# The sums over four states in the body's scan move from the decay's tile to a tile of their own

## The chip, the cores and the metric

The kernel runs on one core of a Trainium2 chip, in one launch. The metric is device time in microseconds (us), the median of several runs; lower is better. The core's engines work in parallel and wait for each other through semaphores: TensorE (PE; its weight loads are listed apart as PEld), VectorE (DVE), ScalarE (ACT), GpSimd (POOL), and SyncE (SP), whose queue issues all DMAs of this kernel. Each engine and each queue works in the order in which the program lists its instructions.

## What is computed

Two layers of a perceiver-like stack over 8 batches of 64 rows of width 512, in float32, with a context of 1601 rows per batch. The scan that the change touches is the second block, a state space model ("mamba"):

```python
    x = x + _L0_xattn_ref(_layernorm(x, axis=-1), ctx_4096, ...)
    x = x + _L0_attn_ref(_layernorm(x, axis=-1), ...)      # the scan
    x = x + _L0_ffn_ref(_layernorm(x, axis=-1), ...)
    x = x + _L1_xattn_ref(_layernorm(x, axis=-1), ctx_4096)
    x = x + _L1_attn_ref(_layernorm(x, axis=-1), ...)
    x = x + _L1_ffn_ref(_layernorm(x, axis=-1), ...)
```

and within `_L0_attn_ref`:

```python
        def step(state, inp):
            dt_t, B_t, C_t, u_t = inp
            dA = jnp.exp(dt_t[..., None] * A)
            state = state * dA + (dt_t * u_t)[..., None] * B_t[:, None, :]
            y = jnp.einsum('bdn,bn->bd', state, C_t)
            return (state, y)
...
        y = ys.transpose(1, 0, 2) + x * D
```

There are 1024 channels, 16 states per channel and 64 time steps per batch. The sum over states in `y` is what is stored elsewhere after the change.

## The kernel before

**Main stream.** The first cross attention (32 heads, 8 key heads) is most of the work. `x_all` (L527) walks over 64 units, one per batch and key head: keys (`k_ps`, L363), values (`v_ps`, L334), scores (`s_ps`, L385), running maximum on DVE (`mx`, L392, L390, L395), exponentials (DVE L426, ACT L427), weighted values (`o_ps`, L464), their scaling (L476 to L479), and for each pair of batches the output projection (`w_ps`, L521, added on DVE at L524). The keys leave PSUM through ACT L108 and DVE L109.

**Side chains.** The batches are grouped in pairs. When the first attention of a pair is done, a generator for the other five blocks of that pair starts (`chain`): mamba, `ffn`, `xattn1`, `attn1`, `ffn1`. The first three pairs' chains ("body") run beside the main stream; `advance` (L1328) draws from them in proportion to the main stream's progress, so the program text interleaves both. What a body chain records is pinned by `keep_in_program_order` (L65, the line that the profile gives to all of it): an edge places it behind the instruction recorded just before it on its engine. The main stream's own instructions are not pinned. A list scheduler then orders each engine's instructions by a timing model of its own, and gives tiles their buffers, within these edges. The last pair's chain runs after the main stream ("tail"), with other buffers and other code for the scan (`tail` branches); what is left of the third chain runs beside it.

**The body's scan.** `mamba` (L807) holds 8 tiles of 128 channels; `scan(c, sh, bc)` (L895) takes one tile `c` and four of the 16 states, so a chain has 4 x 8 = 32 scans, and the three body chains 96. One scan does, on tiles of 128 x 512 (four states x two batches x 64 steps):

1. ACT: four exponentials into `da`, the decay (L899); POOL: a memset of the first step of `da` (L900);
2. POOL: `h` = B x du (L905), with B from `bc`, which a DMA spreads over the partitions once for every eight scans (L885, one buffer);
3. DVE: the scan itself, over `da` and `h` into `h` (L909, TENSOR_TENSOR_SCAN);
4. DVE for even `c`, POOL for odd `c`: `h` times C (L911);
5. DVE: the sum over the four states (L914, TENSOR_REDUCE) into `y`, which is the first quarter of `da`;
6. DVE: the update of `u` with `y` (L915, SCALAR_TENSOR_TENSOR, shown as `lv<-lv,a` or `lv<-lv,c_Dp,a`).

`da` and `h` come from the tag `a2`, five buffers of 2 KB per partition in the body's pool `ca`. The profile shortens `a2` to `a`. The normalised and transposed input of mamba is also an `a2` tile and is read until the gates at the end of mamba. A buffer is given to the next tile when the last reader or writer of the old one is done, which for `da` is step 6 and for `h` step 5.

**The tail's scan** has no `y` tile; it adds the states on PE (L956).

The third chain's `xattn1` reads the context again: scores L1036 with loads of `ctxT` (L1033), transposes L1074, values L1092 with loads of `ctxN` (L1087, L1089).

Of the kernel before, what the change touches and what calls it, by code (L numbers as in the profile page):

```python
# [16 lines left out]
P = 128  # L17
D = 512
NC = 4
T = 64  # L20
# [22 lines left out]
CPLAN = (0, 1, 2, None, None, 3)  # L43
AVPLAN = ((), (), (0, 1, 2, 3), (4, 5, 6, 7), (8, 9, 10, 11), (12,))
EXPLAN = ((0,), (1, 2), (3,), (4, 5), (6,), ())
BUFS = {"a2": 5, "lv": 3, "bc": 1, "xpad": 1, "b2": 5, "b4": 2, "w2": 3, "xr": 2}
BUFS_TAIL = {"a2": 6, "du": 2, "bc": 2, "xpad": 4, "s4": 11, "kb": 3, "b2": 8, "b4": 3, "w2": 12, "xr": 2}


# [29 lines left out]
class Kernel:  # L79
# [13 lines left out]
    def sb(self, tag, shape, dt=FP, bufs=None, pool=None):  # L93
        if pool is None:
            pool, bufs = self.ca if tag in MAMBA_TAGS else self.cp, bufs or self.bufs.get(tag)
            if tag in REST and self.tp and not self.tail:
# [710 lines left out]
    def mamba(self, gi, x, xo):  # L807
# [40 lines left out]
        sm = self.sb("sm", [64, P], bufs=1)  # L848
# [36 lines left out]
        def bcast(sh):  # L885
            bc = self.sb("bc", [P, 2, HS, 2, T])
            for a in range(2):
                r = a * NST + sh * HS
                nc.sync.dma_start(
                    out=bc[:, a].rearrange("p s b t -> p (s b t)"),  # L890
                    in_=self.bc_s[gi][r : r + HS].rearrange("r t -> (r t)")[None, :].to_broadcast([P, HS * P]),
                )
            return bc

        def scan(c, sh, bc):  # L895
            da = self.sb(self.td, [P, HS, 2, T])
            for s in range(HS):
                k = sh * HS + s
                nc.scalar.activation(da[:, s], dt[:, c], AF.Exp, scale=self.A[:, c, k : k + 1])  # L899
            nc.gpsimd.memset(da[:, :, :, 0:1], 0.0)  # L900
            du = dus[:, c]
            if sh == 0:
                nc.gpsimd.tensor_tensor(du, dt[:, c], u[:, c], ALU.mult)
            h = self.sb(self.ts, [P, HS, 2, T])
            nc.gpsimd.tensor_tensor(h, bc[:, 0], du[:, None].to_broadcast([P, HS, 2, T]), ALU.mult)  # L905

            yield 1
            hf, df = h.rearrange("p s b t -> p (s b t)"), da.rearrange("p s b t -> p (s b t)")
            nc.vector.tensor_tensor_scan(hf, df, hf, 0.0, ALU.mult, ALU.add)  # L909
            yield 1  # L910
            (nc.gpsimd if c % 2 else nc.vector).tensor_tensor(h, h, bc[:, 1], ALU.mult)  # L911
            yield 1
            y = da[:, 0]
            nc.vector.tensor_reduce(y.rearrange("p b t -> p (b t)"), h.rearrange("p s b t -> p (b t) s"), AX.X, ALU.add)  # L914
            nc.vector.scalar_tensor_tensor(u[:, c], u[:, c], self.Dp[:, c : c + 1] if sh == 0 else 1.0, y, ALU.mult, ALU.add)  # L915
            yield 1

        wps = None
        if tail:
# [18 lines left out]
            for c in range(NCH):  # L938
                du = self.sb("du", [P, 2, T])
                nc.gpsimd.tensor_tensor(du, dt[:, c], u[:, c], ALU.mult)  # L940
                for k0 in range(0, NST, CS):
                    da = das[k0 // CS % 2]
                    for s in range(CS):
                        nc.scalar.activation(da[:, s, :, 1:], dt[:, c, :, 1:], AF.Exp, scale=self.A[:, c, k0 + s : k0 + s + 1])
                    bc, o = bcs[k0 // HS], k0 % HS
# [17 lines left out]
        else:  # L963
            for sh in range(nh):
                bc = bcast(sh)
                for c in range(NCH):
                    yield from scan(c, sh, bc)
# [332 lines left out]
    def run(self):  # L1300
        nc, tc, ctx = self.nc, self.tc, self.ctx
        nc.scalar.preload_act_table_set("natural_log_exp_and_others")
        self.setup(bufs=BUFS, accb=2, hs=4, tail=False, ahead=1, **TAGS)
        self.pc = ctx.enter_context(tc.tile_pool(name="pc", bufs=2, space=PSUM))
# [74 lines left out]
GROUPS = {8: [2, 2, 2, 2], 2: [2]}  # L1379
SPAN = [3.1,3.1,2.6,0.2]  # L1380
PREP_END = 2.8
MAMBA_TAGS = ("a2", "lv", "bc", "xpad", "sm")
FFN_TAIL = (("l", 0), ("l", 1), ("a", 0), ("l", 2), ("a", 1), ("d", 0), ("a", 2), ("d", 1), ("d", 2))
REST = {"w2":8,"b4":3}
OTB = 1
# [114 lines left out]
```

## Time and profile before

| what | us |
| --- | --- |
| median of three runs | 2729.16 (2728.2 to 2729.43) |
| the profiled execution, its own time | 2721.08 |
| its span, first to last instruction | 2719.3 |
| first body scan, first exponentials to last sums | about 752 to 1010 |
| second body scan | about 1397 to 1691 |
| third body scan | about 2028 to 2313 |
| last rows of the main stream's w_ps on PE | 2422 |

The mean granted clock of TensorE over the profiled execution is 0.977 of full speed. In the tables, "idle before, releaser" is the time for which an engine did nothing before an instruction, with the event that ended it; "x" is a number of instructions. A row of the view of time has its start and its length in us. The costliest instructions of the body's scan are, per instruction: TENSOR_TENSOR_SCAN 1603 ns (96 of them), TENSOR_REDUCE 1068 ns (96), the product with C on DVE 1115 ns (48), the update 487 ns (72) or 743 ns (24, those with D), and an exponential 392 ns on the page (384, all three chains).

### The profile page before, as it was taken

To read this page: it belongs to the slowest core of one execution; us is meant where nothing else is said; L and a number is where in the kernel's file an instruction comes from. 1 tells how busy PE (TensorE), PEld (TensorE's weight loads), DVE (VectorE), ACT (ScalarE), POOL (GpSimd) and SP (SyncE) were. 2 spreads that over 40 slices of the span, in tenths; PEclk is the share of its full clock that TensorE was granted. 3 is DMA by queue.
4 is the path that set the end of the run, shared out by engine and by line. 5 is a ranking of instruction groups with operands and counts; after the bars stand their busy time and mean duration, and the time that the engine had idled before them with its cause. 6 is when DMAs were issued, how large, how long until landed. Compare 5 with 4: busy or idle time off the path is not lost.

```text
span 2719.3 us, 43920 instructions
## 1 busy us (share of the span) xinstructions
PE 2565.7 (94%) x16288; PEld 2273.7 (84%) x16288; DVE 1746.8 (64%) x2843; ACT 1352.6 (50%) x3128; POOL 1171.4 (43%) x1123
## 2 busy tenths in 40 slices
PE   7999999999998899999999988999999998986888
PEld 6999999889887899978988987997897898964644
DVE  4544345577688886545568689544668879457854
ACT  4444554445565554544455554544555455445543
POOL 3212434464588643422357346421249445114610
PEclk9999999999999999999999998999999999997999
DMA  9544446665665234665234443565342463476575
GB/s 308 153 141 153 138 144 228 200 204 178 214 218 188 75 121 159 211 184 174 88 109 134 152 136 106 185 206 186 116 133 80 128 187 113 148 256 201 195 264 188
DMA packets 302934, 455.59 MB, mean 168 GB/s; under 512 B 80248, under 2 KB 179576, under 8 KB 298240
## 3 DMA queue, kind: packets, MB, share of 16 engines
q1 hardware_dynamic: 302720, 452.79, 52.2%
q8 instruction: 128, 2.10, 0.3%
q14 instruction: 86, 0.70, 0.1%
HBM read 380.23 MB, written 72.48 MB: 166 GB/s over the span
## 4 chain that ended last, share of the span: by engine, by line
PE 47%; DVE 11%; DMA 4%; POOL 3%; issue 3%; ACT 2%; POOLq 0%; DVEq 0%; ACTq 0%; SPq 0%
PE v_ps L334 10%; PE k_ps L363 10%; PE o_ps L464 6%; PE s_ps L385 5%; DVE a L65 4%; PE w_ps L521 2%; PE acc L819 2%; PE acc L777 2%; PE acc L774 1%; PE acc L1092 1%; PE acc L1036 1%; POOL a L65 1%; POOL ss L452 1%; DVE acc L953 1%; PE acc L1178 1%
## 5 line engine op out<-in xcount | busy, mean ns | idle before, releaser
L363 PE MATMUL k_ps<-cxb,wk 128*128 128x384 f32 x2304 | 473.5, 348 | 36.4 <-DVE kt L109 12.6
L334 PE MATMUL v_ps<-wv,cxb 128*128 128x256 f32 x3456 | 474.1, 283 | 7.4 <-DVE mx L392 3.9
L334 PEld LDWEIGHTS v_ps<-wv,cxb 128*128 128x128 f32 x3456 | 441.8, 190 | 28.9 <-issue 13.6
L363 PEld LDWEIGHTS k_ps<-cxb,wk 128*128 128x128 f32 x2304 | 406.8, 192 | 56.3 <-DVE kt L109 14.3
L385 PE MATMUL s_ps<-q,kt 128*128 128x256 f32 (+1 forms) x2496 | 414.5, 299 | 8.6 <-DVE mx L392 7.2
L464 PE MATMUL o_ps<-S,v 128*128 128x256 f32 (+1 forms) x1664 | 413.6, 381 | 2.6 <-DVE rw L479 1.7
L388 ACT COPY S<-s_ps 128x512 f32<-128x512 f32 (+1 forms) x448 | 242.5, 554 | 252.6 <-PE s_ps L385 249.0
L385 PEld LDWEIGHTS s_ps<-q,kt 128*128 128x128 f32 (+1 forms) x2496 | 342.0, 185 | 30.3 <-DVE mx L392 8.5
L392 DVE TENSOR_TENSOR mx<-s_ps,mx 128x512 f32<-128x512 f32 x256 | 175.4, 685 | 297.5 <-ACT S L388 297.2
L452 POOL TENSOR_TENSOR ss<-ss,S 128x512 f32<-128x512 f32 x254 | 356.6, 1404 | 14.9 <-ACT S L427 0.3
L429 POOL TENSOR_TENSOR ss<-S,S 128x512 f32<-128x512 f32 x64 | 84.0, 1312 | 640.0 <-ACT S L427 639.9
L464 PEld LDWEIGHTS o_ps<-S,v 128*128 128x128 f32 (+1 forms) x1664 | 299.4, 190 | 41.6 <-issue 5.6
L426 DVE TENSOR_TENSOR S<-S,m_ps 128x512 f32<-128x512 f32 (+1 forms) x448 | 257.5, 641 | 36.2 <-PE m_ps L412 35.4
L108 ACT ACTIVATE kt<-k_ps,c_bk 128x384 fp32r<-128x384 f32 (+1 forms) x256 | 151.8, 593 | 246.2 <-PE k_ps L363 245.4
L427 ACT ACTIVATE S<-S 128x512 f32<-128x512 f32 (+1 forms) x448 | 247.6, 600 | 41.4 <-DVE S L426 41.0
L109 DVE SCALAR_TENSOR_TENSOR kt<-k_ps,c_bk,kt 128x384 fp32r<-128x384 f32 (+1 forms) x256 | 160.9, 629 | 156.2 <-ACT kt L108 155.0
L337 ACT COPY v<-v_ps 128x256 f32<-128x256 f32 (+1 forms) x416 | 152.1, 368 | 195.8 <-PE v_ps L334 192.7
L334 PE MATMUL v_ps<-wv,cxt 128*128 128x256 f32 (+1 forms) x1536 | 211.3, 286 | 5.1 <-DVE mx L392 5.1
L334 PEld LDWEIGHTS v_ps<-wv,cxt 128*128 128x128 f32 (+1 forms) x1536 | 194.6, 176 | 17.3 <-issue 5.9
L363 PE MATMUL k_ps<-cxt,wk 128*128 128x450 f32 x768 | 179.3, 376 | 0.0
L65 DVE TENSOR_TENSOR_SCAN a<-a,a 128x512 f32<-128x512 f32 x96 | 153.9, 1603 | 32.2 <-POOL a L65 32.0
L65 ACT ACTIVATE a<-lv,c_A_log 128x128 f32<-128x128 f32 x384 | 122.8, 392 | 85.8 <-DVE a L65 84.8
(358 smaller groups left out, 3951.3 us busy)
## 6 DMA issues: line engine op xcount, KB each, us to landing
wo<-d_wo SPq DMA_DIRECT2D x96, 512.0 KB, 5.6
wk<-d_wk SPq DMA_DIRECT2D x63, 512.0 KB, 4.3
wv<-d_wv SPq DMA_DIRECT2D x31, 1024.0 KB, 5.7
cst<-in_ctxT_dram SPq DMA_DIRECT2D x96, 192.0 KB, 2.7
b<-in_ctxN_dram SPq DMA_DIRECT2D x36, 512.0 KB, 3.8
d_q<-q_t SPq DMA_DIRECT2D x32, 512.0 KB, 4.3
q<-d_q SPq DMA_DIRECT2D x64, 256.0 KB, 3.0
d_wo<-b SPq DMA_DIRECT2D x32, 512.0 KB, 2.9
```

The source lines that it names most:

```text
L65: return lambda *a, **k: self.tc.keep_in_program_order(f(*a, **k))
L109: eng.scalar_tensor_tensor(lo, src, bias, hi.bitcast(FP), ALU.add, ALU.subtract)
L334: nc.tensor.matmul(ps[:r], lhsT=cx[:, a, c, o : o + r], rhs=w[:, m, c, :], start=k == 0, stop=k == 11)
L337: nc.scalar.copy(vt[:r], ps[:r])
L363: nc.tensor.matmul(ps[:, :wd], lhsT=w[:, a, c, :], rhs=cx[:, m, c, :], start=k == 0, stop=k == 11)
L385: nc.tensor.matmul(sp[:r, gi, :], lhsT=kt[:, a, o : o + r], rhs=q[:, m, :], start=k == 0, stop=k == 2)
L388: nc.scalar.copy(s[:r, :n], sp[:r, :n])
L392: nc.vector.tensor_tensor(mx, sp, S[0] if len(S) == 1 else mx, ALU.max)
L426: nc.vector.tensor_tensor(sv, sv, ps[:r, 1:2].to_broadcast([r, w, 256]), ALU.add)
L427: nc.scalar.activation(sv, sv, AF.Exp, scale=ISC)
L452: nc.gpsimd.tensor_tensor(ss, ss, S[n], ALU.add)
L464: nc.tensor.matmul(ps[:, 0], lhsT=self.v[(b, j, t)][:r, hc : hc + P], rhs=S[t // 2][:r, t % 2], start=t == 0, stop=t == NT - 1)
```

## The change

The sum of step 5 goes into a tile `y` of its own, 128 x 2 x 64, with two buffers in the pool `ca`; the update reads it from there. `da` is then last read by the scan itself. The amount and form of the instructions stay as they are. The tail is not edited. The order that the scheduler finds, and the addresses, may differ anywhere after the first scan.

```diff
-BUFS = {"a2": 5, "lv": 3, "bc": 1, "xpad": 1, "b2": 5, "b4": 2, "w2": 3, "xr": 2}
+BUFS = {"a2": 5, "y": 2, "lv": 3, "bc": 1, "xpad": 1, "b2": 5, "b4": 2, "w2": 3, "xr": 2}
...
             (nc.gpsimd if c % 2 else nc.vector).tensor_tensor(h, h, bc[:, 1], ALU.mult)
             yield 1
-            y = da[:, 0]
+            y = self.sb("y", [P, 2, T])
             nc.vector.tensor_reduce(y.rearrange("p b t -> p (b t)"), h.rearrange("p s b t -> p (b t) s"), AX.X, ALU.add)
...
-MAMBA_TAGS = ("a2", "lv", "bc", "xpad", "sm")
+MAMBA_TAGS = ("a2", "y", "lv", "bc", "xpad", "sm")
```

`MAMBA_TAGS` lists the tags that come from the pool `ca`.

## The prediction

> **What bounds the kernel now.** I read the page first, then the stretches by engine, then the waits and the order of time inside the scans, and the end last. The page's first and clock lines:
>
> ```profile
> span 2719.3 us, 43920 instructions
> PE 2565.7 (94%) x16288; PEld 2273.7 (84%) x16288; DVE 1746.8 (64%) x2843; ACT 1352.6 (50%) x3128; POOL 1171.4 (43%) x1123
> PEclk9999999999999999999999998999999999997999
> ```
>
> TensorE (PE) is busy 94% of the span, and the work on it is the same before and after. So the edit can only move PE's idle time, 2719.3 − 2565.7 = 154 us, and the time lost to a lower clock. The waits of PE named in the view of time add up to 23 us in the first body scan (740 to 1010 us), 17 us in the dense half of the second (1600 to 1695), 15 us in the third (2028 to 2312), and some 70 us after 2400. Stretches of 10 us in the second scan and of 20 us near the end (columns: PE, weight loads, DVE, ACT, POOL busy with instructions, granted clock, DMA share, GB/s):
>
> ```profile
> 1610.00:1620.00 10.00, 5.34 (x30) 4.88 (x29) 6.83 (x7) 2.26 (x6) 4.16 (x6) 0.90 0.73 262
> 1660.00:1670.00 10.00, 4.99 (x19) 4.60 (x20) 9.93 (x12) 4.83 (x15) 3.94 (x5) 0.66 0.10 26
> 1670.00:1680.00 10.00, 7.49 (x51) 6.67 (x51) 10.00 (x15) 5.32 (x15) 4.40 (x5) 0.97 0.00 0
> 2420.00:2440.00 20.00, 14.08 (x89) 10.36 (x85) 8.59 (x25) 7.92 (x22) 0.42 (x6) 0.74 0.98 334
> ```
>
> Where the scan is dense, VectorE (DVE) is full and PE half idle; in the fourth row DMA is full. The waits of 1600 to 1695 us, and the rows around one sum over states:
>
> ```profile
> ACT a L65 <- DVE a L65: 37.6, 13, 7.5
> DVE a L65 <- POOL a L65: 9.0, 5, 3.5
> PE k_ps L363 <- DVE mx L392: 4.7, 1, 4.7
> 1616.09 1.22 DVE L65 TENSOR_TENSOR_SCAN a<-a,a 128x512 f32<-128x512 f32 x1
> 1617.23 1.01 DVE L65 TENSOR_REDUCE a<-a 128x128 f32<-128x512 f32 x1
> 1618.15 0.68 DVE L392 TENSOR_TENSOR mx<-s_ps,mx 128x512 f32<-128x512 f32 x1
> 1618.75 0.28 DVE L65 SCALAR_TENSOR_TENSOR lv<-lv,a 128x128 f32<-128x128 f32 x1
> 1618.95 1.04 DVE L65 TENSOR_REDUCE a<-a 128x128 f32<-128x512 f32 x1
> 1620.03 1.12 DVE L65 SCALAR_TENSOR_TENSOR lv<-lv,a 128x128 f32<-128x128 f32 x1
> 1618.33 1.28 ACT L65 ACTIVATE a<-lv,c_A_log 128x128 f32<-128x128 f32 x4 [7.52 <-DVE a L65]
> ```
>
> ACT's four exponentials start at 1618.33, when the sum (TENSOR_REDUCE) of 1617.23 ends. That is the wait which the edit touches. But PE's 4.7 us ended with mx at 1618.15, which stood on DVE behind the scan and the sum: PE lost by DVE's queue.
>
> **The change, part by part.** *Removed and added instructions:* none; 96 sums and 96 updates (SCALAR_TENSOR_TENSOR of lv) read and write another tile. y takes two buffers of 512 B.
>
> *(a) The decay's buffer comes free earlier: −3 us, bounds −6 and 0.* Of the five a2 buffers one holds the normalised input to the end of mamba, so two pairs of da and h are left. In the order of the old program 87 first exponentials take a buffer that a sum frees, and 93 products h = B·du one that DVE's update or scan frees. In the new one 91 exponentials take a buffer freed by a scan or update, and 66 products one freed by a sum. The exponentials may thus start a product and a sum earlier: 2.2 us (mean 1115 + 1068 ns), and h an update earlier. ACT's 37.6 us is no gain by itself: the chain of waits from 1595 to 1700 us holds ACT's exponentials once, for 1.29 us. What h's lateness costs DVE there is 9.0 us in five waits, of which 3.50 and 3.22 end with the load of bc, which stays single; 2.3 us remain. In 2200 to 2312 DVE waits 7.3 us for POOL, 2.6 of it behind bc. I take half of 2.3 + 4.7, about 3; all of it is 7, cut to 6 since PE does not lose every one.
>
> *(b) h meets the update on DVE: +2 us, bounds 0 and +4.* The update takes 0.28 us alone and 1.12 in the row above, where POOL runs too; 96 updates cost 52.8 us, 26 over 96 × 0.28, while the sums stay at 1.07 throughout. A product bound by the buffer used to start 0.08 us after the update; now it may start after the sum, and where a row of the main stream lies between sum and update (58 of 96 in the new order) the update can find POOL at work. I count some eight bound products in the trace; half of them at 1.0 us is 4, half of that 2.
> The Trainium skill, "SBUF — State Buffer" (Who interferes with whom), says that a DVE instruction with two SBUF inputs contends with a GpSimd instruction that reads SBUF, and that the one that issues first blocks the other, a reduction never. That speaks against the edit; the row's 0.84 us and the sums' constancy agree. By the page each late update would pay the rest of a 1.28 us product, 8 × 1.28 = 10 us by an estimate from it; the sum stays with the rows.
>
> *(c) The scheduler packs the scans closer: +8 us, bounds 0 and +12.* This is the largest term. With earlier buffers the built order puts side work ahead of main rows. Up to the second chain's end the order on DVE shifts by 0 to 7 rows, then by about 10, and in the third scan by 5 to 14. To price it I cut the 32 sums of a scan into groups of four and count the main rows of DVE in each, at the page's means. A group's own DVE work is 4 × (1.603 + 1.068 + 0.487) + 2 × 1.115 = 14.9 us. The main rows L392, L426, L109, L390, L395, L405, L476, L477, L479, L524 make 869 us over some 2340 us of the main stream, so PE at full pace asks for 0.37 us of them per us. A group with M us of main rows lasts at least M + 14.9 and lets PE do M/0.37 of work; below M = 8.7 PE starves. Old order, second scan: groups of 6.3 and 5.0 lose 4.1 and 6.4, together 10.5 (the trace shows 17 of idle PE there); third scan: one of 4.0 loses 8.1 (trace: 9 of idle PE from 2200 on). So the count is of the right size. New order: second scan 5.0 and 3.7, losing 6.4 and 8.6; third 5.3 and 2.7, losing 5.9 and 10.3. Together 31.2 against 18.6: +12.6. Group borders are arbitrary, and what stands beside the last group of 2.7 is a fuller one of 9.3, so I take two thirds, +8, and 0 if neighbours even it out.
>
> *(d) The end of the main stream: 0, bounds −10 and +6.* The third chain arrives earlier. In the old order the first context attention (batch 4) has 28 score matmuls L1036 around the last rows of w_ps, and its transposes L1074 and values L1092 behind them; in the new one 13 transposes and 12 of 13 pairs of values stand before the start of the last chain. Three loads of ctxT and four of ctxN, some 3.3 MB, move ahead of the last wo on SP's queue. At 334 GB/s that is 9.9 us of a DMA that is full from 2420 on, a wait of this kind being
>
> ```profile
> 2463.48 9.07 DMA b<-in_ctxN_dram
> 2429.76 1.56 PE L1036 MATMUL acc<-b,b 128*64 128x194 f32 x8 [2.14 <-DMA b<-in_ctxT_dram]
> ```
>
> Against it: the last wo now queues on SP behind a ctxN load that waits for its buffer, and PE has two pairs of values between the two parts of the last w_ps; two loads at about 3 us (3.38 and 3.72 in the chain of waits) make +6. DVE's last sum of w_ps, and with it the whole last chain, waits for that. I see no reason to prefer one: 0.
>
> Sum: −3 + 2 + 8 + 0 = +7. The profiled execution took 2721.1 us, its span 2719.3, and would become 2728. The runs' median is 2729.2, 8.1 above the profiled one; on that scale **2736 us**.
>
> **Rivals.** *Faster, by the end and the buffers:* −4 of (a) and −6 of (d), with (c) evened out: 2729 − 10 = 2719. For it: the full DMA from 2420 to 2480, and PE's clock of 0.74 there, at which any matmul moved forward gets cheaper. Against: the last chain's own sixteen W_in loads remain, and the second batch's ctxT loads move into the place.
> *No change:* PE is 100% busy between the scans, the dense groups only exchange losses, and the freed buffer is off the path (ACT is in the chain once in 105 us): 2729. Against it: the third scan's order moves by up to 14 rows, and nothing makes PE's losses cancel exactly. That the edit does not do what it says belongs here; the order says that it does.
> *Slower by (c), the forecast's own side:* in place, the last four sums of the third scan; it decides once fewer than 8.7 us of main rows stand in four sums.
>
> **How the numbers follow.** 0.2%, 5.5 us, is about what a measurement tells from no change. Slower 0.50: (c) is counted from the order and only its size is open; its own range is 2735 to 2746. Faster 0.27: (d)'s lower half together with (a). No change 0.23: (c) and (d) against each other. The range runs from 2719, the faster rival, to 2746: −3 + 4 + 12 + half of (d)'s 6, 16 above, rounded to 17. Beyond lie the rest of −10 with −6, and all bad ends at once, some 0.2.
>
> **What would show it.** (a): ACT's waits for DVE between the body's scans fall by a third or more, and exponentials start with the end of a scan. (b): the 96 updates' sum is 50 to 57 us. (c): PE's waits behind DVE in the last 60 us of the third scan grow from 9 us to 14 or more; if they do not, (c) is wrong and the forecast with it. (d): L1074 and L1092 of the third chain stand before the last w_ps; from the start of its last rows (2422.0) to the end the old profile has 297 us, and a figure below 289 makes the faster rival true.

## The result, and the profile after

The changed kernel takes 2744.66 us (median of five runs, 2740.4 to 2746.79), the kernel before 2729.16 (median of five, 2723.94 to 2729.54) beside it: a ratio of 1.0065, 95% interval 1.0046 to 1.0083, or 15.5 us more where 7 were forecast. The profiled execution has a span of 2745.0 us. First the page (span, busy time and share of the engines, granted clock in 40 slices):

```profile
span 2745.0 us, 43930 instructions
PE 2570.2 (94%) x16288; PEld 2283.1 (83%) x16288; DVE 1748.2 (64%) x2843; ACT 1353.5 (49%) x3128; POOL 1174.8 (43%) x1123
PEclk9999999999999999999999999999999999997898
```

PE does the same 16288 matmuls in 4.5 us more of busy time; the other 21 us of the longer span are idle time of PE. In the clock's last six slices two stand at 8 where the kernel before has 9.

Then the second scan's dense part, the waits of the kernel after from 1595 to 1705 us (engine and line, what it waited for: us in total, times, longest):

```profile
ACT a L65 <- DVE a L65: 27.8, 9, 6.0
ACT a L65 <- DVE y L65: 7.9, 7, 2.3
PE m_ps L412 <- DVE mc L405: 5.3, 1, 5.3
PE k_ps L363 <- DVE mx L392: 3.7, 1, 3.7
```

The wait of ACT that the edit aims at is still there: 27.8 behind the scan and 7.9 behind the sum, 35.7 together, against 37.6. The exponentials of the whole body show the same (groups of the page: busy, mean ns, idle before with its releasers; first before, then after):

```profile
L65 DVE TENSOR_TENSOR_SCAN a<-a,a 128x512 f32<-128x512 f32 x96 | 153.9, 1603 | 32.2 <-POOL a L65 32.0
L65 ACT ACTIVATE a<-lv,c_A_log 128x128 f32<-128x128 f32 x384 | 122.8, 392 | 85.8 <-DVE a L65 84.8
```
```profile
L65 DVE TENSOR_TENSOR_SCAN a<-a,a 128x512 f32<-128x512 f32 x96 | 152.6, 1591 | 38.3 <-POOL a L65 35.6
L65 ACT ACTIVATE a<-lv,c_A_log 128x128 f32<-128x128 f32 x384 | 122.8, 392 | 87.5 <-DVE a L65 72.8
```

ACT waits 87.5 us where it waited 85.8, and DVE's scans wait 38.3 us where they waited 32.2. Over all profiles of the two orders ACT's wait is 84.7 to 89.3 us before (six) and 81.6 to 90.3 after (seven), the scans' 31.9 to 32.4 and 36.8 to 38.5. The buffer comes free earlier, but the next exponentials are listed earlier too: in the third chain on average 13 rows of ACT's other work (2 to 22), in the first two about one.

The updates, by form, first before, then after:

```profile
L65 DVE SCALAR_TENSOR_TENSOR lv<-lv,a 128x128 f32<-128x128 f32 x72 | 35.0, 487 | 1.1
L65 DVE SCALAR_TENSOR_TENSOR lv<-lv,c_Dp,a 128x128 f32<-128x128 f32 x24 | 17.8, 743 | 0.2
```
```profile
L65 DVE SCALAR_TENSOR_TENSOR lv<-lv,y 128x128 f32<-128x128 f32 x72 | 39.0, 543 | 1.0
L65 DVE SCALAR_TENSOR_TENSOR lv<-lv,c_Dp,y 128x128 f32<-128x128 f32 x24 | 21.3, 891 | 0.3
```

Together 60.3 us, 52.8 before.

**Where the time went.** Every profile holds the same 13088 matmul records of the main stream. Between the orders some of them stand a few places apart, but up to each point used here the same ones, by line, have run, so two executions can be compared at the same matmul. The points are named by their time in the kernel before: the 7521st record is at 1365 us, the 9234th at 1686, the 11772nd at 2167. The last three stretches run to the last w_ps, to the end of the last chain's values (L1092), and to the end of the span. Of the kernels of the section below, those that have the order of the kernel before (or after) in a stretch are put with it; in brackets, how many profiles.

| stretch, us | order of before | order of after | difference of the means |
| --- | --- | --- | --- |
| start to 765 | 762.5 to 768.1 (8) | 764.2 to 768.6 (10) | +0.5, within the scatter |
| to 1010: first scan | 243.3 to 253.9 (8) | 241.0 to 247.9 (10) | -4.8, less than the scatter |
| to 1365 | 354.8 to 356.5 (8) | 354.9 to 356.6 (10) | +0.2, within the scatter |
| to 1686: second scan | 320.4 to 322.0 (8) | 318.8 to 322.0 (10) | -0.6, within the scatter |
| to 2024: between the scans | 337.5 to 339.4 (8) | 340.3 to 341.7 (10) | +2.9 |
| to 2167: third scan, first half | 141.6 to 143.5 (6) | 147.5 to 148.8 (7) | +5.1 |
| to 2351: rest of the third scan | 182.9 to 184.7 (6) | 187.5 to 188.9 (7) | +4.5 |
| to the last w_ps | 71.7 to 72.9 (4) | 77.4 to 81.7 (4) | +7.1 |
| last chain to its last values | 203.8 to 205.0 (4) | 199.9 to 200.9 (4) | -4.0 |
| the last 90 us | 91.7, 93.5 (2) | 99.3, 100.0 (2) | +7.0 |

The sum is 18, near the 15.5 us of the times (13.5 when both kernels were run again). The second scan loses nothing. From 1686 us on each order's stretches come again within 5 us and the two orders do not overlap, so those differences belong to the order. They add up to 22.6 us, more than the times give; the rest is the first scan. There eight executions of the old order fall into two groups (243.3, 243.6, 245.0, 245.8 and 250.9, 253.8, 253.8, 253.9), and the ten of the new order all lie below the second group. That the new order gains some 5 us there on average would fit, but it is not shown.

The way to the last w_ps, before and after (columns: PE, weight loads, DVE, ACT, POOL busy with instructions, granted clock, DMA share, GB/s):

```profile
2351.00:2423.00 72.00, 67.32 (x414) 57.97 (x412) 37.18 (x79) 29.14 (x64) 13.04 (x11) 1.00 0.50 158
```
```profile
2365.00:2445.00 80.00, 74.69 (x445) 59.23 (x444) 37.13 (x78) 30.69 (x68) 13.12 (x11) 0.96 0.54 172
```

PE has 31 pieces and 7.4 us more to do there, and about as much idle time (4.7 and 5.3 us).

### The profile page after: what moved, and what is told of

It reads as the page before. It is cut to its first block, busy times and chain, and to the rows that moved or that the text cites. A ratio compares the mean times of both kernels' runs of the same rounds, so it can differ in the third digit from the quotient of the medians.

```text
span 2745.0 us, 43930 instructions
## 1 busy us (share of the span) xinstructions
PE 2570.2 (94%) x16288; PEld 2283.1 (83%) x16288; DVE 1748.2 (64%) x2843; ACT 1353.5 (49%) x3128; POOL 1174.8 (43%) x1123
## 4 chain that ended last, share of the span: by engine, by line
PE 69%; DVE 15%; DMA 6%; POOL 4%; issue 4%; ACT 3%; SPq 0%; POOLq 0%; DVEq 0%; ACTq 0%
PE v_ps L334 16%; PE k_ps L363 15%; PE o_ps L464 9%; PE s_ps L385 8%; DVE a L65 4%; PE w_ps L521 3%; PE acc L274 3%; PE acc L819 2%; PE acc L1036 2%; PE acc L1092 2%; PE acc L774 2%; POOL a L65 2%; PE acc L777 1%; DVE y L65 1%; DVE b L65 1%
## 5 line engine op out<-in xcount | busy, mean ns | idle before, releaser
L388 ACT COPY S<-s_ps 128x512 f32<-128x512 f32 (+1 forms) x448 | 242.0, 553 | 250.9 <-PE s_ps L385 246.8
L65 DVE TENSOR_TENSOR_SCAN a<-a,a 128x512 f32<-128x512 f32 x96 | 152.6, 1591 | 38.3 <-POOL a L65 35.6
L65 ACT ACTIVATE a<-lv,c_A_log 128x128 f32<-128x128 f32 x384 | 122.8, 392 | 87.5 <-DVE a L65 72.8
```

What stands on the lines that cost most here:

```text
L65: return lambda *a, **k: self.tc.keep_in_program_order(f(*a, **k))
L388: nc.scalar.copy(s[:r, :n], sp[:r, :n])
```

## The experiments

A ratio is always to the kernel before, run beside it, with its 95% interval. "NoSync edge" means that the scheduler must list one instruction behind another on the same engine; nothing waits for it on the chip.

**Holding the context attention of batch 4.** The last w_ps comes 22 us late in the profile after, and 12 scores, 13 transposes and 8 values of the third chain stand ahead of it that stood behind it. An edge holds them back:

```diff
-   nc.tensor.transpose(tp[:r, t - t0, :], ...)
+   self.hold(b, nc.tensor.transpose(tp[:r, t - t0, :], ...))   # b == 4 is noted
...
+   for ins in self.held:      # after the last w_ps is recorded: NoSync edges
+       self.tc.add_manual_dep(ins.ins, last.ins.name, dep, reason="behind")
```

> The kernel after, with one edge more for the order: on TensorE the transposes L1074 of the third chain's first context attention (batch 4), and with them its values L1092, stand behind the last w_ps. In the changed kernel 13 transposes and 8 values stand before it (3.1 and 12.5 us of matmul in its trace). Theory 'end': what stands before the last w_ps adds its length there, because PE is full, and the stretch from the last w_ps to the end (297 us before, 300 after) is set by the last chain itself and has room for it. It expects about 10 us less than the 2744.7 of the changed kernel: 2735, between 2731 and 2739. Theory 'scan': the 15.5 us come from DVE's denser queue in the second and third scan, which this edge does not touch: 2741 to 2749. Theory 'full end': the stretch after the last w_ps is filled by PE's work, so work held comes back there: 2744 to 2755.

> The kernel after, with the scores L1036 of batch 4 held behind the last w_ps as well, all 28 of them (12 stand ahead through the change, 16 did so before it). Theory 'end': 10 us as in the run with the values held, and some 12 more for 28 scores of 0.9 us each, which overlap with others: about 2722, between 2714 and 2729, faster than the kernel before. Theory 'scan': 2741 to 2749. Theory 'full end': 2750 to 2765, as 40 us of matmul are added to the end.

> The kernel before with the same edge: batch 4's context attention behind the last w_ps. Only the 16 scores that stand ahead of it in the kernel before are moved (some 14 us of matmul). Theory 'end': 5 to 12 us less than 2729: 2717 to 2724. Theory 'scan': no change, 2726 to 2733, as no scan is touched. Theory 'full end': 2733 to 2745.

Measured: 2745.98 us, 1.0074 (1.0051 to 1.0096) with the values held; 2735.33, 1.0029 (1.0016 to 1.0042) with the scores too; 2726.76, 0.9991 (0.9974 to 1.0009) for the kernel before with the hold. Holding the values brings nothing: the way to the last w_ps falls from 79 to 77.7 us, the last chain's way to its values grows from 200.4 to 204.1. With all held the first falls to 67.6, but the last 90 us become 105.9. So the theory "end" has the right sign where scores are held, and is wrong that the stretch after the last w_ps has room for anything. None of the three theories explains all three runs.

**The tile without the early release; one part of the chains alone; both kernels again.** In the first the update reads a zero of `da` as its scalar in 72 of 96 scans:

```diff
-   nc.vector.scalar_tensor_tensor(u[:, c], u[:, c], self.Dp[...] if sh == 0 else 1.0, y, ALU.mult, ALU.add)
+   nc.vector.scalar_tensor_tensor(u[:, c], u[:, c], self.Dp[...] if sh == 0 else da[:, 0, 0, 0:1], y,
+                                  ALU.mult if sh == 0 else ALU.add, ALU.add)
```

> The kernel after with its tile y, but the update of 72 of the 96 scans reads a zero of da as its scalar (add 0 in place of multiply by 1), so that da is held to the update as in the kernel before; the result is the same. In the built order four-scan groups lack main rows about as before the change (by the count of the forecast 10.3 and 9.3 us, before 10.5 and 8.1, after 14.9 and 16.2), no transpose and no value of batch 4 stands before the last w_ps, 12 scores more than before do. If the early release, through the order that it lets the scheduler find, is the cause ('end' and 'scan' alike): 2729 plus at most 6 to 8 for the scores, 2729 to 2738, 'scan' alone 2727 to 2732. If the new tile itself, its address or the sum written elsewhere, costs the time: 2741 to 2748.

> The run with the tile of its own and da held to the update, once more for a second profile without other edges: its time was 11 us over the kernel before, its groups beside the sums about as before. Theory 'the end is 8 us for every such order': the stretch from the last values to the last matmul is again 95 to 98 us (before 88 and 90), and the delay at the last w_ps from 1365 us on is again 8 to 10 us. The time lies within 2734 to 2746.

(The label of the second is wrong: it is the same kernel as the first, as its text says.) For the parts:

```diff
-   y = self.sb("y", [P, 2, T])
+   y = self.sb("y", [P, 2, T]) if gi == 2 else da[:, 0]     # third chain alone; gi < 2: first two
```

> The change in the third chain alone (chains 1 and 2 keep the sum in da). Up to the second scan's end the order is that of the kernel before. In the third scan the built order has groups of 2.0 and 6.0 us of main rows beside four sums (count of the forecast: 16.2 us lost, 8.1 before), and 12 scores and 8 transposes of batch 4 move ahead of the last w_ps. Theory 'third scan and end' (the third scan's denser end and what its earlier end puts ahead of the last w_ps make up all of the loss): 2740 to 2746. Theory 'second scan too' (a third or more of the 15.5 us is made in the second scan and what follows it): 2732 to 2739.

> The change in chains 1 and 2 alone; the third chain keeps the sum in da. Up to the second scan's end the order is that of the kernel after; in the third scan four sums never have less than 7.4 us of main rows beside them (count: 2.8 us lost, 8.1 before), and 12 scores of batch 4 but no transposes move ahead of the last w_ps. Theory 'third scan and end': 2722 to 2733. Theory 'second scan too': 2733 to 2740.

> The changed kernel a second time, for a second profile: the parts of the delay at the last main matmul (idle time of PE, side work done by then, time of the main stream's own matmuls) and the length of the end show which of them come again. If the end after the last w_ps is longer by a property of the order, it is again 296 to 301 us; the third scan's stretch that took 67.2 us (59.7 before) is again 66 to 68. The time stays within 2740 to 2748.

> The kernel before a second time, for a second profile: if its end of 293 us is a property of the order, it is again 290 to 295; if it varies from execution to execution by 8 us or more, the end tells nothing about the change. The time stays within 2718 to 2738.

| run | ratio | 1365 to 2167 | to 2351 | to last w_ps | to last values | last 90 us |
| --- | --- | --- | --- | --- | --- | --- |
| tile, da held (2 profiles) | 1.0049 (1.0031 to 1.0067) | 803.7, 801.3 | 185.2, 184.6 | 78.5, 78.3 | 204.1, 206.3 | 100.2, 99.2 |
| third chain alone | 1.0054 (1.0036 to 1.0072) | 809.5 | 186.4 | 74.6 | 204.8 | 100.1 |
| first two alone | 1.0046 (1.0030 to 1.0062) | 805.9 | 184.3 | 76.5 | 203.8 | 101.6 |
| after again | 1.0055 (1.0033 to 1.0077) | 808.3 | 188.3 | 77.4 | 199.9 | 100.0 |
| before again | 2735.1 us, one time | 803.4 | 183.4 | 72.9 | 205.0 | 93.5 |

With `da` held to the update in these 72 scans, the way from 1365 to 2351 us costs in sum about what it cost before (988.9 and 985.9 us; 983.6 to 986.8 in six profiles of the old order), so no cost of the new tile itself shows there. But the sum hides two parts: the second scan's stretch is 313.6 and 315.0 us, some 6 below both orders, and the third scan's first half 149.6 and 147.6, as long as in the kernel after. So this run, a third order, does not show that the third scan's loss comes through the early release. Its time, 2738.72 us, lies between the ranges of its two theories.

Each partial change loses nearly as much as the whole, 12 to 15 us, and the one place where all of them lose alike is the last 90 us: 99 to 102 where the kernel before has 91.7 and 93.5. The third chain alone lay within the first theory's 2740 to 2746, the first two alone within the second's 2733 to 2740: neither theory holds both, since neither looks at the last 90 us.

**The order of the last 90 us.** From the last chain's attn1 on, instructions of PE, DVE and ACT get the order of the other kernel (230, 71 and 59 of them where the old order is put into another kernel, 226, 66 and 54 where the new one is put into the kernel before); all before that point stays.

```diff
     Kernel(ctx, tc, ins, out).run()
+    ...                                      # per[e]: the instructions of engine e as the program has them
+    for e, ranks in ORDER.items():           # the other kernel's order of these instructions
+        for a, b in zip(ranks, ranks[1:]):   # NoSync edges
+            tc.add_manual_dep(per[e][b], per[e][a].name, dep, reason="order")
```

> The kernel after, unchanged up to the start of the last chain's last-but-one block (attn1, L1148); from there on the last 230 instructions of PE, 71 of DVE and 59 of ACT stand in the order of the kernel before. From the end of the last chain's values (L1092) to the last matmul the profiles have 83.7 and 85.5 us for the kernel before and 91.6 for the kernel after. Theory 'order of the end' (the difference is made by how the scheduler interleaves chain 3's last block with chain 4's): that stretch becomes 83 to 87 us and the time 2741 to 2745 less 6 to 8, 2733 to 2738. Theory 'the end is set by data and the chip': the stretch stays 90 to 93 us, the time 2740 to 2746.

> The reverse: the kernel before up to the same point, and from there on the order of the kernel after. Theory 'order of the end': the stretch from the last values to the last matmul becomes 90 to 93 us, and the time 2727.5 plus 6 to 8, 2733 to 2736, with not one instruction of the scan moved. Theory 'data and chip': 2724 to 2731.

> The kernel after with batch 4's context attention held behind the last w_ps (2735.3 alone) and the old order of the end. In that run the stretch from the last values to the last matmul was 97.8 us. Theories 'end' (work ahead of the last w_ps) and 'order of the end' together: 2735.3 less 8 to 12, 2723 to 2727, the level of the kernel before; what is left over it belongs to the scans. Theory 'data and chip': 2733 to 2737.

> The change in chains 1 and 2 alone (2738.8 by itself), with batch 4's context attention held and the old order of the end. By the profile of the run without the two edges its scans cost some 3 to 4 us at the last main matmul, the work ahead of the last w_ps 4, the end 8. Theories 'end' and 'order of the end' together: 2720 to 2728, perhaps below the kernel before; if the scans alone set the time, 2735 to 2740.

Measured: after with the old end 2733.56 us, 1.0025 (1.0010 to 1.0041), its last stretch 91.5 us; before with the new end 2739.65, 1.0042 (1.0027 to 1.0057), its last stretch 105.9, with every scan untouched. This shows the order of the end as a cause of its own, in both directions, worth 8 to 11 us. The hold with the old end: 2734.21, 1.0021 (1.0009 to 1.0032), last stretch 105.0, against 105.9 with the hold alone: the old end brought nothing there, and the 2723 to 2727 expected were missed. Perhaps that order suits a third chain that is as far as in the kernel before, and not one that was held; no run tests this. The first two chains alone, held, with the old end: 2729.19, 1.0005 (0.9993 to 1.0017), no difference to the kernel before, and a little above the 2720 to 2728 expected.

What it looks like. The timeline of PE in the kernel after (start and length in us; the last values end at 2645.7):

```profile
2661.70 0.66 PE L1282 MATMUL acc<-ident,b 128*128 128x128 f32 x4 [0.51 <-DVE b L1272]
...
2670.47 0.60 PE L1148 MATMUL acc<-ident,b 128*128 128x128 f32 x4
...
2687.66 1.00 PE L1205 MATMUL acc<-ident,b 128*128 128x128 f32 x4 [3.93 <-DVE b L1197]
...
2695.84 0.60 PE L1282 MATMUL acc<-ident,b 128*128 128x128 f32 x4
...
2711.51 0.75 PE L1282 MATMUL acc<-ident,b 128*128 128x128 f32 x3 [3.29 <-DVE b L1272]
2712.70 1.09 PE L727 MATMUL acc<-ident,b 128*128 128x128 f32 x4 [0.45 <-DVE b L144]
2715.70 10.05 PE L1259 MATMUL acc<-s,b 128*128 128x512 f32 x48
```

and with the old end (the last values end at 2649.7):

```profile
2671.99 0.66 PE L1148 MATMUL acc<-ident,b 128*128 128x128 f32 x4 [1.69 <-DVE b L1145]
...
2680.45 0.66 PE L1282 MATMUL acc<-ident,b 128*128 128x128 f32 x4
...
2688.12 0.66 PE L1205 MATMUL acc<-ident,b 128*128 128x128 f32 x4
...
2702.08 0.60 PE L1282 MATMUL acc<-ident,b 128*128 128x128 f32 x4
...
2707.33 0.60 PE L727 MATMUL acc<-ident,b 128*128 128x128 f32 x4
2710.13 10.07 PE L1259 MATMUL acc<-s,b 128*128 128x512 f32 x48
```

L1148, L1205 and then L727 and L1259 are the last chain's steps, one behind the other: the second transposes of attn1, its first transposes of attention weights, and the start of ffn1. L1282 begins a block of chain 3's ffn1 (four transposes and 16 matmuls L774 and L777). With the old end L1148 comes 22.3 us after the last values, L1205 38.4, L727 57.6; with the new one 24.8, 42.0 and 67.0. The new order puts chain 3's first block ahead of L1148 and its second between the last chain's L1205 steps; and its third, which waits 3.29 us for DVE, directly ahead of L727; the old one has the first behind the last chain's third score (six records of L1178), and the second after the last L1205, where PE would otherwise wait for the last chain's layernorm. PE took its queue in order in all these rows, so a block ahead of a ready step delays the last chain: in the kernel before with the new end, the first block moves L1148 from 23.1 to 30.3 us after the last values.

The stretches of the last 90 us, before and with the new end (columns: PE, PEld, DVE, ACT, POOL busy with instructions, granted clock, DMA share, GB/s):

```profile
2628.00:2719.30 91.30, 72.04 (x330) 43.99 (x328) 45.22 (x87) 33.08 (x67) 8.27 (x9) 0.96 0.59 203
```
```profile
2629.20:2735.10 105.90, 78.81 (x330) 48.17 (x330) 44.29 (x87) 33.16 (x67) 7.94 (x9) 0.85 0.51 175
```

The same 330 pieces of PE take 6.8 us more at a clock of 0.85 than at 0.96, and PE is idle 7.8 us longer (27.1 against 19.3). The kernel after, with its own end and with the old one:

```profile
2645.70:2745.00 99.30, 73.25 (x319) 44.79 (x318) 42.62 (x84) 33.48 (x67) 7.99 (x9) 0.90 0.50 169
```
```profile
2649.70:2741.20 91.50, 71.42 (x319) 43.29 (x318) 44.46 (x84) 33.27 (x67) 8.26 (x9) 0.93 0.55 183
```

Here 6.0 of the 7.8 us are idle time (26.1 against 20.1), and 1.8 the same pieces at the lower clock. In the timeline the slow rows follow the waits: behind the 3.29 us at 2711.51, rows of L774 and L777 with 512 columns take 0.78 and 0.63 us, and 0.40 two us later. No run holds one and changes the other. The Trainium skill, "TensorE: Matmul & The Clock Gate" (Part 1: The HAM clock gate), says that the clock is gated by how busy PE has lately been, so that idle gaps lower it; both pairs of lines agree with that, as the stretch with more idle time has the lower clock.

**One block, and what the scans cost by themselves.** One edge in the kernel after puts chain 3's first `down` (L1282) behind the last chain's sixth score; the third chain alone and the first two alone get the old end.

```diff
+    for i in k.first_down:     # four transposes L1282 of chain 3; NoSync edges
+        tc.add_manual_dep(i.ins, k.score.ins.name, dep, reason="behind")
```

> The kernel after with one edge more: chain 3's first 'down' in ffn1 (four transposes L1282, and behind them its pairs L774 and L777) stands on PE behind the sixth score L1178 of the last chain, as in the kernel before; all else is left to the scheduler. In the new end this block stands ahead of the last chain's second transposes L1148, which start 30.3 us after the last values in place of 23.2. Theory 'one block ahead': the 7.1 us come back, the time is that of the run with the whole old end (ratio to the kernel before 1.0025) within 3 us: 2732 to 2738. Theory 'many small shifts': less than half of the 8 to 9 us comes back: 2738 to 2744.

> The change in the third chain alone, with the old order of the end. What is left over the kernel before is then the third scan and the way to the last w_ps: its profile without the old end was 10 to 11 us late there, its end 8 us longer. Theory 'the end is 8 us for every such order, the rest is the third scan': 4 to 7 us over the kernel before, ratio 1.0015 to 1.0026. If the third scan costs nothing: 0.9990 to 1.0010. If the old end brings nothing here: 1.004 to 1.006.

> The change in chains 1 and 2 alone, with the old order of the end. Theory 'the end is 8 us': 2 to 5 us over the kernel before, ratio 1.0007 to 1.0018 (its profile is 8 us late at the last w_ps, 4 of them work done ahead that shortens the end). If the second scan's new order were as dear as the third's: 1.0020 to 1.0035. If the old end brings nothing here: 1.004 to 1.006.

One edge: 2737.69 us, 1.0032 (1.0015 to 1.0048), as "one block ahead" expected; its last stretch is 94.8 us in one profile, so 5 of the 7 us that the end lost are this block and what the scheduler lists behind it. Third chain alone with the old end: 2738.52, 1.0037 (1.0020 to 1.0054), between the 1.0015 to 1.0026 expected where the end is worth 8 us and the 1.004 to 1.006 where it is worth nothing; last stretch 92.2. First two alone with it: 2729.08, 1.0014 (0.9997 to 1.0030), last stretch 90.8.

The body's loss is made mostly in the third scan's stretch (2024 to 2351 us), whichever chains are changed: 335.0 to 337.0 us with all three, 336.3 and 336.6 with the third alone, 330.5 to 331.8 with the first two alone, 324.9 to 327.1 before. So the third scan loses some 5 us even where its own code is the old one. That the third chain alone costs no less than all three with the old end (1.0025) would fit a first scan that the new order makes shorter, as the third chain alone keeps the old order there; it is not shown, and the intervals overlap.

**The same block moved in the kernel before.** There its transposes stand behind the third of the last chain's eight scores, and its matmuls around the fourth to the sixth; the edge puts it behind the eighth.

> The kernel before with one edge for the order of the end: chain 3's first 'down' in ffn1 (L1282, then 16 matmuls L774 and L777) stands behind the eighth score L1178 of the last chain, and no longer between its sixth and seventh pair. In the profile of the kernel before those matmuls take PE from 33.2 to 38.3 us after the last values, and the last chain's first L1205 comes at 39.3. Theory 'one block ahead' (what stands ahead of the last chain's attn1 on PE is added to the end, chain 3 has room): 3 to 5 us less than the kernel before, ratio 0.9982 to 0.9990, the stretch from the last values to the end 87 to 89 us (91.7 and 93.5 before). Rival 'chain 3 then ends last': no change or slower, 0.9995 to 1.002.

> The same edge together with batch 4's context attention held behind the last w_ps (0.9991 alone). If chain 3 still has room in the end: 0.997 to 0.9985. If chain 3, now later by both edges, ends last: 1.000 to 1.003.

Measured: 2743.55 us, 1.0057 (1.0039 to 1.0074), some 14 us slower with only the end's order changed, last stretch 104.3 us; with the hold 2730.34, 1.0008 (0.9995 to 1.0021). Theory "one block ahead" was wrong: pushed back, the block falls between the last chain's L1205 steps, and the second block directly ahead of L727, where it waits 5.44 us for DVE; L1259 starts 72.0 us after the last values where it started at 61.2. So there is no room on either side, and "less of chain 3 ahead" is no rule by itself. No run was measurably faster than the kernel before.

## Why the prediction was right or wrong

The direction was right; the size was half. The step that failed is (d), "The end of the main stream: 0, bounds -10 and +6". From the first scan to the end of the third, the stretches add up (-4.8, +0.2, -0.6, +2.9, +5.1, +4.5) to the +7 that (a) to (c) gave together, in part by luck, as other places and waits make it up; the end of the main stream adds 10 more.

*(d).* It looked at the order as far as the last w_ps and the start of the last chain. What it saw there is in the trace: the transposes and values do stand ahead, and the way to the last w_ps is 7.1 us longer, of which the last chain gets 4.0 back before its values end. It left out the last 90 us, where chain 3's ffn1 and the last chain share PE and where the two orders differ as well: +7.0 in the profiles of both kernels, 8 to 11 in the times of the two runs that exchange the end. Together +10 where 0 was put and +6 was the bound. The mark set for it, the time from the last rows of w_ps to the end, is some 300 us, not below 289: the faster rival is refuted. It expected matmuls moved forward to shorten the end; they shortened it by 4 us and the new order took 7.

*(c).* +8 by the count of main rows beside the sums, bounds 0 and +12. Measured are +2.9 us between the second and the third scan and +5.1 and +4.5 in the third, against -0.6 in the second: 11.9 us, at the upper bound. About 6 us of it are idle time of PE (43.1 against 36.8 in the first two profiles) and 3 are side work done ahead. In times, with the old end and the first scan's stretch included, it is 5 to 7 us (1.0025). So the size is about right, but not the mechanism. The count put some 4 us of its 12.6 into the second scan, whose dense part was not worse (PE's idle time 12.4 us, 14.1 before, in the stretch to 1671). For the first two chains alone it gave 5 us less than before in the third scan; measured are 5 more. And its mark, PE's waits behind DVE in the last 60 us of the third scan growing from 9 to 14 us, did not come: they are 4.8 us before and 5.1 after. PE's idle time there does grow by about 5, from 4.7 to 9.4 us, but the wait that came on top stands behind ACT:

```profile
2292.07 1.28 ACT L65 ACTIVATE a<-lv,c_A_log 128x128 f32<-128x128 f32 x4 [2.90 <-DVE a L65]
...
2293.72 0.64 ACT L337 COPY v<-v_ps 128x256 f32<-128x256 f32 x2
2294.13 3.25 PE L363 MATMUL k_ps<-cxb,wk 128*128 128x384 f32 x9 [4.35 <-ACT v L337]
```

The exponentials wait on ACT for the buffer that the scan frees, the main stream's copy of v stands behind them in ACT's queue, and PE waits 4.35 us for that.

*(a).* -3 was forecast, with ACT's waits down by a third. They did not fall, and DVE waited longer for `h`. In the third chain the scheduler, handed a free buffer earlier, lists the exponentials 13 rows earlier, where they wait again; that (c) comes of this alone is not shown, as the third scan also loses where its own release is the old one. Whether the first scan gained (-4.8 us, within the scatter) stays open.

*(b).* +2, bounds 0 and +4, and 50 to 57 us for the updates. Seven profiles of the new order have 60 to 64 us, six of the old 51 to 53: some 11 more on DVE. The step halved its eight collisions, and that was wrong: of the 72 updates without D, 7 or 8 start while POOL computes a product B x du in three profiles of the old order, and 15 or 16 in four of the new, eight more. Nearly every update of over 0.45 us ends 0.14 to 0.16 us after the POOL instruction that ran at its start. The Trainium skill, "SBUF — State Buffer" (Who interferes with whom), says that of the two the one that issues first blocks the other, and the trace agrees. The estimate of 10 us that the prediction worked out from it is nearer to the measured 11 than its rows' 2. In the runs that hold `da` the updates, 72 of them in another form, take 67 us while the body's stretches are in sum as before, so this DVE time need not reach the end.

*Rivals.* "No change" failed because losses did not cancel; "slower by (c)" was right in kind, and is about 5 to 7 of the 15.5 us.

Open: what the lower clock at the end costs by itself, whether the new order gains in the first scan, and which wait makes the third scan's loss in the kernels with a part of the change.

## What to carry to other kernels

Where a scheduler decides the order, compare the orders down to the last instruction, and most closely where the longest chain runs without cover: a block of another chain ahead of it on an in-order queue can delay it by the block's length, and the same block later can cost as much. To separate an edit from the reshuffle that it sets off, put the old order back in one stretch with ordering edges, and the new order into the old kernel. And split a stretch before calling it unchanged: a gain in one part can hide a loss in the next. A buffer that comes free earlier is no gain unless the wait for it was the last one.

## What the runs showed of the hardware

The first body scan took 243.3 to 253.9 us in eight executions of one order, in two groups some 8 us apart, while the next 355 us came again within 1.7 us and the 321 us of the second scan within 1.6: most of the scatter of this kernel arises in that one stretch. The same matmuls at the end took 72.0 us at a granted clock of 0.96 and 78.8 at 0.85. An update on DVE that took 0.26 us alone took up to 3.05 us where POOL was at work, and nearly always ended 0.15 us after POOL's instruction.
